# Four graph layers on one core: the last slot and the drain of layers 0 to 2 written as one list of steps, with the first two attention units of layer 3 inside it

## The chip, the core and the metric

The kernel runs on one core of a Trainium2 chip. The metric is the device time of one execution in microseconds; the median of three runs before the change is 2056.01 us (2053.41 to 2056.41). A compute core has five engines that run beside each other, each through its own list of instructions in order: TensorE (PE, matrix products into PSUM, with its weight loads shown as PEld), VectorE (DVE), ScalarE (ACT), GpSimd (POOL) and SyncE (SP), which here only starts transfers.

## The reference

Input x is 32 graphs of 512 nodes with 64 features, adj a sparse symmetric 512 x 512 matrix. Four layers follow each other, each of the form x = x + layer(relu(layernorm(x))):

```python
# layer 0: h = relu(layernorm(x))
out = h @ w_self + (adj @ h) @ w_neighbor + bias
# layer 1: z = h, then twice
z = relu((adj @ z) @ weights[i])
# layer 2: graph attention with e1_i + e2_j as its scores
Wh = h @ W.T;  e = leaky_relu(e1[:, None] + e2[None, :], 0.2)
out = elu(softmax(where(adj > 0, e, NEG)) @ Wh)
# layer 3: 8 attention heads, then one more attention over all heads
def gat_layer(x, graph, W, b):
    h = x @ W
    s = (h @ h.T) * graph
    s = where(s == 0, -1e16, s)
    return softmax(s) @ h + b
cat = leaky_relu(concat(heads), 0.01)
out = leaky_relu(gat_layer(cat, adj, W_out, b_out), 0.01)
```

Everything is float32.

## The kernel before, in words

All of x lies in SBUF. Work has two parts. **Layers 0 to 2** go by blocks: a block is two graphs, and there are 16 of them (M = 16). **Layer 3** goes by units of two attention matrices: 128 `Heads` units (one graph, two heads) and 16 `Out` units (two graphs), 144 in all.

*Layers 0 to 2.* `slot(k)` (L1134) holds one step of several blocks at once: layer 0 of block k, the first half of layer 1 of block k-2, its second half for block k-3 (`ends`), and of layer 2 the flip and preparation of block k-4 and the scores and products of block k-5. PE, DVE and ACT run in the order in which the code is written, by `manual_schedule`. The names that matter, with the lines where they are in the profile:

- nt (L930): the product with adj, four matmuls of 512 columns, copied out by ACT (L937). One is layer 0's (nt0), two are layer 1's (nt1, then nt1b with z).
- po (L950): products with the small weights (po0, po1a, po1b). z is relu of po1a.
- `centre` (L869, L871) takes off the mean; the square is taken on ACT (L890), its sum on DVE (var, L908), the root on ACT (L915), and `relu` (L894) applies it.
- `Gat` (L959): flip (L318, a transpose, copied to ht at L320), e_ps and wh_ps (L973, L982), their exponentials on ACT (v, q and c, L993 to L999), weigh (L1004), scores (s, L1014), acc and den (L1027, L1036), kept (two copies on ACT, L1046), back (two groups of transposes, den_ps and op_ps, L1058 and L1063), read (L1073 to L1076), exp (e, L1083), and rest (L1089 to L1092), which adds to x and takes the mean and square for layer 3.

In the first slots a set-up step of its own is run at a slot's end (`begun`, L1336): `gat_weights`, edges, masks, `flow_weights`, `scales`, and then checks of adj row by row (`judge_rows`, `count_rows`, `judge`), which lead to the flag that chooses the general form.

Slot 16 is the last. `drain` (L1224) then ends blocks 12 to 15, written by hand, with 36 recorded products of `fill` (L1222), whose result nobody reads, and with the first periods of layer 3's preparation (-10 to -2) between.

*Layer 3.* `period(t)` (L743 and on, made by `planned`) does for each unit a step that depends on its age: the scores s_ps (L391) of rows 2 and 3 of unit t and of rows 0 and 1 of unit t+1; the maxima (L403, which also copy to p_att); the row maximum sent to memory and back to all partitions (top_row, topb: L410, L418, on SP); the shift by it on POOL (L424, L428); the exponential (L437); the join of two rows (L440, DVE); the totals (tot_ps, L458); the products (av, L446); the reciprocals, sent round in the same way (recb); normalise (L495); and the output steps. p_att has a ring of 14 tiles. The ring, the row tiles and the PSUM pools are opened when the pools of layers 0 to 2 are closed. In period 1 the shift runs on DVE.

Of the kernel before, what the change touches and what calls it, by code (L numbers as in the profile page):

```python
# [10 lines left out]
OP = mybir.AluOpType  # L11
# [11 lines left out]
def fast_form(  # L23
# [48 lines left out]
    early = ctx.enter_context(tc.tile_pool(name="early", bufs=1))  # L72
    setup_ctx = ExitStack()
    setup = setup_ctx.enter_context(tc.tile_pool(name="setup", bufs=1))
    adj_p = setup.tile([P, C, C, P], F32, name="adj_p")
# [94 lines left out]
    def scales():  # L170
        own = tiny.tile([P, C], F32, name="own_edge")
        for c in range(C):
            d = row_pair("d")[:, 0, :P]
            nc.vector.scalar_tensor_tensor(
                d, adj_p[:, c, c], 1.0, ident, op0=OP.mult, op1=OP.mult,
                accum_out=own[:, c : c + 1],
            )
        nc.vector.tensor_scalar(sound[:, 2 : 2 + C], own, 1e-20, None, op0=OP.is_gt)
        nc.vector.tensor_scalar(own, own, 1e-20, None, op0=OP.max)

        root = tiny.tile([P, C], F32, name="root")
        nc.scalar.activation(root, own, AF.Sqrt)
        nc.vector.reciprocal(root_d, root)
        nc.vector.tensor_tensor(root_d, root_d, own, OP.mult)
        nc.vector.tensor_tensor(root_d, root_d, root, OP.add)
        nc.vector.tensor_scalar(root_d, root_d, 0.5, None, op0=OP.mult)
        ones = row_pair("ones")[:, 0, :P]
        nc.vector.memset(ones, 1.0)
        ps = acc("urow_ps", [P, N])
        for c in range(C):  # L190
            d = row_pair("d")[:, 0, :P]
            nc.vector.tensor_scalar(d, ident, root_d[:, c : c + 1], None, op0=OP.mult)
            nc.tensor.matmul(
                ps[:, c * P : (c + 1) * P], lhsT=ones, rhs=d, start=True, stop=True
            )
        nc.scalar.copy(urow, ps)
# [3 lines left out]
    def judge_rows(c):  # L200
        both = judged[c] = row_pair("edge")
# [32 lines left out]
    def row_pair(name):  # L234

        return pairs_of[0].tile([P, 2, N], F32, name=name, tag="row")


    acc_of, pairs_of = [], []
# [4 lines left out]
    def judge():  # L244
        counts = sound[:, 2 + C :]
        nc.vector.tensor_scalar(counts, counts, float(N), None, op0=OP.is_equal)
        own = tiny.tile([P, 1], F32, name="own")
        nc.vector.tensor_reduce(own, sound, AX.X, OP.min)
        ps = acc("own_ps", [1, P])
        nc.tensor.transpose(ps, own, ident)  # L250
        nc.vector.tensor_reduce(unsound, ps, AX.X, OP.min)
# [14 lines left out]

    def gat_weights():
# [6 lines left out]
        wa = setup.tile([P, 2], F32, name="wa")  # L274
# [3 lines left out]
        size = tiny.tile([P, 2], F32, name="size")  # L278
        nc.vector.scalar_tensor_tensor(size, wa, -1.0, wa, op0=OP.mult, op1=OP.max)

        pz = acc("size_ps", [P, 2])
# [5 lines left out]

    def flow_weights():
        whT = pairs_of[0].tile([P, H, 2, F], F32, name="whT", tag="row")
# [3 lines left out]
        for k in range(2):  # L293
            nc.scalar.copy(whT[:, :, k], pt)
        pm = acc("m2_ps", [P, H, F])
# [12 lines left out]
        nc.scalar.mul(bh01, pb, 0.01)  # L308
        nc.vector.tensor_reduce(
# [16 lines left out]

    LATE = 7
# [6 lines left out]
    class Pair:  # L334
# [4 lines left out]
        def begin(self):  # L339
            self.p = {}  # L340
# [45 lines left out]
        def scores(self, r):  # L386
            g, x = self.terms()
            ps = ps_s.tile([P, 2, N], F32, name="s_ps", tag="s")
            self.s_ps[r] = ps
            for k in range(2):  # L390
                nc.tensor.matmul(  # L391
                    ps[:, k], lhsT=x[halves(k), r * P : (r + 1) * P], rhs=g[halves(k), :],
# [3 lines left out]
        def maxima(self, r):  # L396
# [3 lines left out]
            self.p[r] = pbuf.tile([P, 2, N], F32, name="p_att")  # L400
            for k in range(2):
                at = k * C + r
                nc.vector.tensor_tensor_reduce(  # L403
                    out=self.p[r][:, k], in0=ps[:, k], in1=flow_neg[:, r], scale=-1.0,
# [10 lines left out]
        def spread_in(self):  # L415
            self.topb = wk.tile([P, 2, N], F32, name="topb")
# [16 lines left out]
        def exps(self, r):  # L433
            to = self.p[r]
            if r % 2:
                to = self.joined = ps_s.tile([P, 2, N], F32, name="e_ps", tag="s")
            nc.scalar.activation(to, self.p[r], AF.Exp, scale=-1.0)  # L437

        def join(self, r):
            nc.vector.tensor_tensor(self.p[r], self.joined, self.p[r - 1], OP.add)  # L440
# [296 lines left out]
    def planned(units, products):  # L737
# [7 lines left out]
        def period(t):  # L745
# [3 lines left out]
            now, ahead = unit(0), unit(-1)  # L749
# [5 lines left out]
            if t != 1:  # L755
                unit(1).shift(0, nc.gpsimd)
                unit(1).exps(0)
            unit(2).totals()
            unit(2).totals_out(1, nc.scalar)
# [3 lines left out]
            if t != 1:  # L763
                unit(1).shift(2, nc.gpsimd)
                unit(1).exps(2)
# [3 lines left out]
            unit(2).totals_out(0, nc.sync)  # L769
# [8 lines left out]
            if t == 1:  # L778
                for r in (0, 2, 1, 3):
                    unit(1).shift(r, nc.vector)  # L780
                    if r < 3:
                        unit(1).exps(r)
# [3 lines left out]
            if t != 1:  # L786
                unit(1).shift(1, nc.gpsimd)
                unit(1).exps(1)
            for j in range(C):
                unit(2).values(j)  # L790
# [5 lines left out]
            unit(1).join(1)  # L796
            if t != 1:
                unit(1).shift(3, nc.gpsimd)
            unit(1).exps(3)
            unit(5).back_pool()  # L800
            unit(-2).make_gs()
            unit(1).join(3)
# [35 lines left out]
    assert not due and len(late) == LATE  # L838
    flow_period = planned(flow, products)
# [10 lines left out]
    with (  # L850
        tc.tile_pool(name="pairs_a", bufs=H + 3) as pairs,
# [83 lines left out]
        def copied(p, tag):  # L935
            t = work.tile([P, N], F32, name=tag, bufs=1 + (tag == "nt1b"))
# [3 lines left out]
        def flipped(h, tag):  # L940
            return pair_transpose(
# [998 lines left out]
```

## Time and profile before

| | us |
|---|---|
| median of three runs | 2056.01 |
| the profiled execution, its time | 2056.54 |
| its span, first to last instruction | 2054.7 |
| PE, DVE busy in the span | 1966.7, 1736.7 |
| POOL, ACT busy in the span | 1446.0, 1321.5 |
| PE, DVE busy of the first 362.2 | 331.2, 277.0 |

The page of the profile gives each engine's busy time for the whole span, then the span in 40 slices of about 51 us, each digit the busy tenths of an engine. Slices 1 to 9 are layers 0 to 2, the rest is layer 3. A second kind of row gives the same for stretches of one's own choice. A third lists instructions of one engine in order of time, with idle time ahead of one in brackets and who ended it. The clock row (PEclk) is the share of TensorE's full clock that was granted.

### The profile page before, as it was taken

Reading aid. Unit: us, or ns where it says so; the run is one execution under the profiler, and the core shown is the slowest. Engines: PE = TensorE matmul, PEld = TensorE weight load, DVE = VectorE, ACT = ScalarE, POOL = GpSimd, SP = SyncE. Lnnn points to the kernel's source line nnn. Section 1 sums busy time; section 2 is a strip of 40 time slices with the busy share of each in tenths; the row PEclk is TensorE's granted clock in tenths of the full one; section 3 lists DMA queues with packets and bytes.
Section 4 is the critical chain, followed back from the end, with each engine's and each line's share of the span. In section 5 each row is a group of like instructions: output and inputs, shape, how many; then the busy total and the mean of one; then the engine's idle time right before and its main releaser. Section 6 shows DMA issues by size and latency. Waiting matters only on the chain.

```text
span 2054.7 us, 29214 instructions
## 1 busy us (share of the span) xinstructions
PE 1966.7 (96%) x9374; PEld 738.0 (36%) x9374; DVE 1736.7 (85%) x4107; ACT 1321.5 (64%) x2008; POOL 1446.0 (70%) x834
## 2 busy tenths in 40 slices
PE   7999999887999999999999999999999999999995
PEld 4555555432333333333333333333333333333332
DVE  5688887678889898888898888888888888888994
ACT  3444444445676777677676777777777776776674
POOL 2000000005898989898999999898898988889996
PEclk9999999999999999999999999999999999999998
DMA  4000000002222333223332323232322222222233
GB/s 122 1 1 1 1 1 1 1 0 53 79 74 71 82 79 80 79 74 79 79 79 75 84 79 79 69 84 74 76 72 78 74 71 77 79 74 76 72 83 80
DMA packets 185875, 128.05 MB, mean 62 GB/s; under 512 B 124984, under 2 KB 130272, under 8 KB 185584
## 3 DMA queue, kind: packets, MB, share of 16 engines
q1 hardware_dynamic: 166480, 125.30, 22.9%
q10 hardware_dynamic: 18720, 0.59, 0.5%
q8 instruction: 76, 1.25, 0.3%
q14 instruction: 87, 0.71, 0.1%
q0 software_dynamic: 512, 0.20, 0.1%
HBM read 119.48 MB, written 5.37 MB: 61 GB/s over the span
## 4 chain that ended last, share of the span: by engine, by line
PE 75%; DVE 8%; POOL 6%; ACT 5%; DMA 4%; issue 2%; SPq 0%; ACTq 0%; POOLq 0%; DVEq 0%
PE s_ps L391 22%; PE av L446 20%; PE tot_ps L458 6%; PE y_ps L576 5%; POOL p_att L424 5%; PE gT_ps L621 5%; PE nt_ps L930 4%; PE g_ps L558 3%; PE acc L1027 3%; DVE s L1014 2%; DMA topb<-top_row 2%; PE den L1036 1%; DVE p_att L403 1%; PE po L950 1%; DVE p_att L440 1%
## 5 line engine op out<-in xcount | busy, mean ns | idle before, releaser
L424 POOL TENSOR_TENSOR p_att<-p_att,topb 128x1024 f32<-128x1024 f32 x429 | 1008.0, 2381 | 0.0
L403 DVE CUSTOM_DVE_ANT_0 p_att<-s_ps,flow_neg 128x512 f32<-128x512 f32 x1152 | 726.1, 686 | 99.8 <-PE s_ps L391 98.2
L391 PE MATMUL s_ps<-g,hx 64*128 64x512 f32 x2048 | 516.3, 613 | 16.8 <-DVE p_att L440 14.8
L428 POOL TENSOR_TENSOR p_att<-p_att,topb 128x512 f32<-128x512 f32 x286 | 360.4, 1281 | 168.8 <-DMA topb<-top_row 112.5
L437 ACT ACTIVATE p_att<-p_att 128x1024 f32<-128x1024 f32 x288 | 304.8, 1059 | 164.4 <-POOL p_att L428 83.9
L440 DVE TENSOR_TENSOR p_att<-e_ps,p_att 128x1024 f32<-128x1024 f32 x288 | 338.7, 1198 | 31.1 <-ACT e_ps L437 30.5
L437 ACT ACTIVATE e_ps<-p_att 128x1024 f32<-128x1024 f32 x288 | 292.9, 1029 | 79.7 <-POOL p_att L424 74.2
L391 PEld LDWEIGHTS s_ps<-g,hx 64*128 64x128 f32 x2048 | 175.3, 186 | 329.8 <-DVE top L403 174.1
L446 PE MATMUL av<-p_att,hd 128*64 128x512 f32 x1024 | 269.7, 605 | 0.5 <-DVE o_att L495 0.3
L446 PE MATMUL av<-p_att,hn 128*64 128x512 f32 x1024 | 263.3, 592 | 0.0
L1138 POOL TENSOR_TENSOR x<-x,bias_b 128x512 f32<-128x512 f32 x16 | 20.4, 1277 | 292.3 <-DVE hn L871 292.3
L594 DVE SCALAR_TENSOR_TENSOR cat<-y_ps,bh,cat 128x512 f32<-128x512 f32 x256 | 180.1, 745 | 14.2 <-ACT cat L586 12.8
L570 ACT COPY g<-g_ps 128x512 f32<-128x512 f32 x128 | 131.7, 1137 | 85.8 <-PE g_ps L558 85.7
L586 ACT ACTIVATE cat<-y_ps,bh 128x512 f32<-128x512 f32 x256 | 161.4, 682 | 36.4 <-PE y_ps L576 35.7
L458 PE MATMUL tot_ps<-p_att,ones 128*32 128x512 f32 x1152 | 156.4, 608 | 4.0 <-DVE p_att L440 4.0
L576 PE MATMUL y_ps<-o_att,wh_sb 64*128 64x512 f32 x512 | 137.3, 594 | 0.0
L621 PE MATMUL gT_ps<-cat,wo_sb 128*64 128x512 f32 x512 | 131.6, 592 | 0.0
L446 PEld LDWEIGHTS av<-p_att,hn 128*64 128x64 f32 x1024 | 73.9, 137 | 145.9 <-issue 145.9
L446 PEld LDWEIGHTS av<-p_att,hd 128*64 128x64 f32 x1024 | 62.4, 136 | 165.8 <-issue 134.2
L495 DVE TENSOR_TENSOR o_att<-av,recb 128x512 f32<-128x512 f32 x144 | 99.1, 688 | 26.5 <-DMA recb<-rec_row 22.7
L930 PE MATMUL nt_ps<-adj_t,hn 128*128 128x512 f32 x256 | 118.8, 608 | 0.8 <-DVE hn L894 0.8
L464 ACT COPY tot<-tot_ps 128x512 f32<-128x512 f32 x144 | 83.2, 578 | 32.3 <-PE tot_ps L458 31.5
(193 smaller groups left out, 2088.0 us busy)
## 6 DMA issues: line engine op xcount, KB each, us to landing
topb<-top_row SPq DMA_DIRECT2D x288, 256.0 KB
recb<-rec_row SPq DMA_DIRECT2D x288, 128.0 KB
out_dram<-y SPq DMA_DIRECT2D x32, 128.0 KB
x<-in_x_dram SPq DMA_DIRECT2D x3, 1024.0 KB
top_row<-top SPq DMA_DIRECT2D x144, 4.0 KB
parts<-tot SPq DMA_DIRECT2D x144, 4.0 KB
parts<-tot ACTq DMA_DIRECT2D x144, 4.0 KB
rec_row<-rec_flow SPq DMA_DIRECT2D x144, 4.0 KB
```

The costliest lines, as they stand in the source:

```text
L391: nc.tensor.matmul(ps[:, k], lhsT=x[halves(k), r * P : (r + 1) * P], rhs=g[halves(k), :], start=True, stop=True,)
L403: nc.vector.tensor_tensor_reduce(out=self.p[r][:, k], in0=ps[:, k], in1=flow_neg[:, r], scale=-1.0, scalar=BIG, op0=OP.add, op1=OP.min, ac ...
L424: engine.tensor_tensor(self.p[r], self.p[r], self.topb, OP.subtract)
L428: engine.tensor_tensor(p, p, self.topb[:, k], OP.subtract)
L437: nc.scalar.activation(to, self.p[r], AF.Exp, scale=-1.0)
L440: nc.vector.tensor_tensor(self.p[r], self.joined, self.p[r - 1], OP.add)
L446: nc.tensor.matmul(self.av[halves(k), :], lhsT=self.v(k, j) if j % 2 else self.less_next(k, j), rhs=self.p[j][:, k], start=(j == 0), stop= ...
L458: nc.tensor.matmul(ps[q : q + 32, :], lhsT=ones, rhs=self.p[2 * e + 1][:, k], start=True, stop=True,)
L576: nc.tensor.matmul(ps, lhsT=wh_sb[halves(k), 2 * self.i + k, :], rhs=self.o[halves(k), :], start=True, stop=True,)
L594: nc.vector.scalar_tensor_tensor(self.cat[:, k], self.y[k], bh[:, h : h + 1], self.cat[:, k], op0=OP.add, op1=OP.max,)
L621: nc.tensor.matmul(self.gps[halves(k), :], lhsT=wo_sb[:, h, :], rhs=Heads.cat.pop((self.b + k, h)), start=(h == 0), stop=(h == H - 1),)
L930: nc.tensor.matmul(p, lhsT=lhs(k), rhs=adj_t[:, k, :], start=(k == 0), stop=(k == C - 1))
```

## The change

Four things change together.

1. *Set-up in steps.* `gat_weights`, `scales`, `flow_weights` and `judge` are cut where a product needs what DVE or ACT has just made, and the second piece runs a slot later: `gat_sizes` in slot 1, `own_edges` in 2, `roots` in 3, `roots_row` and `flow_squares` in 4, `flow_least` in 5; `judge_counts` in 13, `judge_across` in 14, and the end of `judge` within slot 15.
2. *Inside a slot* the product with z is issued ahead of `back`, and ACT copies nt0 ahead of the square of the second norm.
3. *The list.* Slots run from 0 to 15. What slot 16 and `drain` did is a string of step names, taken one after the other; `fill` is gone. In it stand, of units 0 and 1 of layer 3, the scores (s0 to s3), maxima (m), spread, shifts on POOL (sh), exponentials (ex) and joins (j). Periods -11 to -1 run at the ends of slots 10 to 14. After the list come the totals of unit 0, period 1, its products, period 2, the last root of layer 2, and periods from 3 on; periods leave out what the list did, and in period 3 the shift of rows 1 and 3 is on DVE.
4. *Lasting memory.* Eight of the 14 p_att tiles are held from the start: six tiles `row0` to `row5`, and adj_p as two. Set-up steps use them as scratch. The rows of layer 2 have pools of their own (s: four, c: two, e: one) instead of eleven shared; topb of units 0 and 1 is in adj_t, and their scores are in the PSUM pool of layers 0 to 2, in two banks each.

```diff
+    lasting = [keep.tile([P, 2, N], F32, name=f"row{i}") for i in range(6)]
+    adj_p = keep.tile([P, C, C, P], F32, name="adj_p")
+    lasting += [
+        adj_p.rearrange("p c k q -> p c (k q)")[:, c : c + 2] for c in range(0, C, 2)
+    ]
...
+    EARLY = 2
+    RING = 4 * C - 2
...
+            at = (C * self.at + r) % RING
+            self.p[r] = (
+                lasting[at] if at < len(lasting) else pbuf.tile([P, 2, N], F32, name="p_att")
+            )
...
+            if self.at < EARLY:
+                self.topb = adj_t[:, 2 * self.at : 2 * self.at + 2]
...
-            to = self.p[r]
-            if r % 2:
-                to = self.joined = ps_s.tile([P, 2, N], F32, name="e_ps", tag="s")
+            to = self.joined[r] = self.p[r]
+            if r % 2 and self.at >= EARLY:
+                to = self.joined[r] = ps_s.tile([P, 2, N], F32, name="e_ps", tag="s")
...
+            now, ahead, last = (unit(i) if t - i >= EARLY else nothing for i in (0, -1, 1))
+            summed = unit(2) if t > 2 else nothing
...
             n = make(n2, k - 3)
             if n:
                 n.a()
-                n.square()
                 some.append(n)
             if l0:
                 nt0 = copied(neighbours(lambda c: h0[:, c]), "nt0")
+            if n:
+                n.square()
...
+            if l1:
+                nt1b[k - 2] = neighbours(lambda c: z[:, c, :])
             if u:
                 u.back()
                 turned.append(u)
-            if l1:
-                nt1b[k - 2] = neighbours(lambda c: z[:, c, :])
-            if more:
-                more()
+            for step in more:
+                step()
...
+        LAST = """
+        grow_15 nt1bc_13 flip_12 nt1_14 ht_12 read_10 sc0_11 exp_10 po1b_13 nt1c_14 rest_10
+        e1_12 wh_12 c_12 po1a_14 vq_12 n1_15 s0_0 z_14 osq_10 sc1_11 sq1_15 x_13 acc_11
+        n2_13 var1_15 sq2_13 weigh_12 var2_13 den_11 kacc_11 ovar_10 m0_0 root_0 op_11
+        nt1b_14 sc0_12 kden_11 turn_0 dps_11 relu1_15 nt1bc_14 s1_0 relu2_13 nt1_15 m1_0
+        read_11 sc1_12 exp_11 flip_13 nt1c_15 po1b_14 ht_13 e1_13 rest_11 wh_13 c_13 acc_12
+        vq_13 x_14 osq_11 n2_14 den_12 ovar_11 sq2_14 weigh_13 kacc_12 var2_14 s2_0 kden_12
+        sc0_13 root_1 dps_12 s3_0 po1a_15 m2_0 op_12 z_15 m3_0 nt1b_15 turn_1 relu2_14
+        read_12 sc1_13 flip_14 nt1bc_15 spread_0 s0_1 ht_14 exp_12 po1b_15 e1_14 x_15 acc_13
+        rest_12 c_14 n2_15 osq_12 den_13 sh0_0 kacc_13 ovar_12 sq2_15 m0_1 op_13 kden_13
+        sh1_0 ex0_0 dps_13 var2_15 s1_1 read_13 root_2 s2_1 m1_1 sh2_0 m2_1 s3_1 period_0
+        exp_13 sh3_0 turn_2 ex2_0 wh_14 m3_1 vq_14 relu2_15 spread_1 ex1_0 sc0_14 flip_15
+        ht_15 ex3_0 weigh_14 sc1_14 e1_15 wh_15 c_15 vq_15 sh0_1 rest_13 acc_14 sh1_1 ex0_1
+        weigh_15 osq_13 j3_0 den_14 kacc_14 sh2_1 ovar_13 ex1_1 op_14 sc0_15 kden_14 dps_14
+        sh3_1 ex2_1 sc1_15 ex3_1 read_14 j3_1 exp_14 acc_15 rest_14 den_15 kacc_15 j1_0
+        osq_14 ovar_14 op_15 kden_15 j1_1 dps_15 read_15 exp_15 rest_15 osq_15
+        """
...
+            for step in LAST.split():
+                name, i = step.split("_")
+                do[name](int(i))
...
+            for k, step in (
+                (0, gat_weights), (1, gat_sizes), (1, edges), (2, masks), (2, own_edges),
+                (3, flow_weights), (3, roots), (4, roots_row), (4, flow_squares),
+                (5, flow_least),
+            ):
+                begun[k].append(step)
...
+            for k, some in (
+                (10, (-11, -10, -9)), (11, (-8, -7)), (12, (-6, -5)), (13, (-4, -3)),
+                (14, (-2, -1)),
+            ):
+                for t in some:
+                    begun[k].append(lambda t=t: flow_period(t))
+            for k in range(M):
+                slot(k, begun[k])
+            unfinished = drain()
...
-        for k in range(-1, len(flow) + ROOM):
+        flow[0].totals()
+        flow[0].totals_out(1, nc.scalar)
+        flow[0].totals_out(0, nc.sync)
+        flow_period(1)
+        for j in range(C):
+            flow[0].values(j)
+        flow_period(2)
+        end_of_gat(unfinished)
+        for k in range(3, len(flow) + ROOM):
             flow_period(k)
```

In a step name the number is that of the block, or of the unit for s, m, spread, sh, ex and j. acc and op are one half of values and back, den and dps the other; kacc and kden copy them; x is the end of layer 1; ovar is the sum of rest's square; ending c is the copy of a product (nt1c, nt1bc); osq is the square.

## The prediction

> **What bounds the kernel now.** I read the 40 slices first (how busy each engine is, stretch by stretch), then a table of four stretches, then the waits and the order of time inside the stretches that the change touches.
>
> ```profile
> PE   7999999887999999999999999999999999999995
> PEclk9999999999999999999999999999999999999998
> ...
> 362.23:485.62 123.39, 97.29 (x462) 43.92 (x461) 89.98 (x188) 58.90 (x125) 4.57 (x5) 0.93 0.03 9
> 506.10:2054.70 1548.60, 1517.76 (x7161) 501.23 (x7159) 1354.46 (x3284) 1091.44 (x1563) 1395.67 (x783) 1.00 0.30 77
> ```
>
> The last two rows are stretches, with the busy time of PE, PEld, DVE, ACT and POOL, then clock, DMA share and GB/s. Layer 3 from 506 us on is TensorE's: 1517.8 of 1548.6 us, at full clock. It stays as it is: by the instruction order of both kernels, compared engine by engine with the names of the probability tiles set aside, the periods after the fourth are the same on PE, ACT and SP, and on Pool but for some waits on PE. So the gain must come from the first 510 us. The worst stretch is 362 to 486 (slot 16, drain, first periods of layer 3): PE 79%, DVE 73%, nobody full.
>
> The waits of 100 to 362 us (who waited for whom; us, times, longest), then matmuls in order of time (start, length, operation, and in brackets the idle time before them):
>
> ```profile
> PE den_ps L1058 <- ACT kept L1046: 7.8, 11, 0.7
> PE wh_ps L982 <- ACT nt L937: 6.1, 10, 0.6
> ...
> 58.82 2.00 PE L297 MATMUL m_ps<-whT 128*128 128x64 f32 x16 [1.16 <-ACT whT L294]
> 60.90 5.40 PE L930 MATMUL nt_ps<-adj_t,hn 128*128 128x512 f32 x8
> 67.90 3.60 PE L930 MATMUL nt_ps<-adj_t,hn 128*128 128x512 f32 x8
> 83.34 2.04 PE L193 MATMUL urow_ps<-d,ones 128*128 128x128 f32 x8 [3.63 <-DVE d L192]
> ...
> 398.24 5.40 PE L930 MATMUL nt_ps<-adj_t,z 128*128 128x512 f32 x8 [2.68 <-ACT c L999]
> 485.62 3.79 PE L391 MATMUL s_ps<-g,hx 64*128 64x512 f32 x8 [8.23 <-DVE p_att L440]
> ```
>
> A full slot lasts 25.1 us and holds 23.8 us of PE; the 1.32 us missing are the first two waits. In set-up PE pays twice, once for the gap and once after it: the same nt_ps takes 5.40 instead of 3.60.
>
> **Set-up in steps.** Nothing is computed less; each product is put a slot behind its input. Slot 0's wait for size (1.03 idle, L282) goes. In slot 3, 1.16 idle goes, m_ps drops from 1.95 to about 0.95 (the 16 wh_ps products of 65 columns take 0.95 at full clock), nt_ps gives 1.8: 4.0. In slot 4, 3.63 idle goes, urow_ps falls from 1.84 to 0.9 (eight 128-column products of po1a take 0.9), nt_ps gives 1.7: 6.2. Sum 11.2 us. What took their place is ready: the next slot's DVE steps and copies lie a whole slot before the matmul that needs them. If one were late, its few-us gap returns.
>
> **Slots 5 to 15.** The product with z now stands ahead of back, so the copies of kept (0.59 each) lie under 3.44 us of matmul; the copy of nt0 stands ahead of the square, which waits for DVE. That frees 7.8 + 6.1 = 13.9. Is DVE the next bound? It has 21.9 busy in a judging slot. Its wait for e (2.7 of 25.1 us) shrinks, since nt1b, square, table load and exp start about 1.8 earlier; against it stands up to 0.8 at read, because op_ps comes later. I get 21.9 + 0.8 + 0.35 + 0.45 = 23.5 beside PE's 23.8: just hidden. If that cover fails by 0.3 it costs 8 x 0.3 = 2.4. Judge's 7.7 us wait on DVE goes too, off PE's path. Back on the bill: periods -11 to -1 move into slots 10 to 14. Their hx and g products are about 2 us of PE, and the last g copies (2 x 1.12 on ACT) stand ahead of slot 15's nt1b: about 1 us. The features (12 small ACT operations for each of graphs 0 and 1, 1.06 + 1.05 + 1.28 us, and hd on Pool) fit into ACT's half-empty slots. Net 13.9 - 3.0 = 10.9. So the point that lay at 362.2 comes at 340.1.
>
> **The planned list.** PE: four nt products 13.8, acc and den of five blocks 27.4, four of e and wh 7.7, back 4.7, po 4.5, flips 1.8, units 0 and 1's scores 7.5, g 1.0: 68.4 us. The 36 fill records (17.8 us) go. DVE has more: 89.98 of before, less the five DVE shifts (4.8), the four extra maxima (2.9), unsound, grow and least (1.5), plus two joins (2.4): 83.2 us. So DVE is the floor. I followed the list by hand, each step starting when its engine and inputs allow, lengths from the rows (s x4 2.65, rest 2.87, read 1.1, maxima 1.23, acc 3.6, table load 1.28, about 0.15 a hand-over). Two new orders bind it. The scores tiles s are now four of their own where eleven rows were shared, so the scores of one block wait for den of the block before: in a slot den ends at 281.7 and the scores begin at 292.2, 10 us of cover; in the list sc0_13 follows den_12 by a fraction of a us, and if PE is late there DVE waits with everything queued behind it (read, rest, maxima), us for us. And topb of units 0 and 1 goes into adj_t, which is free only after nt1b_15: spread_0 stands behind it, with 4 us between. DVE stands still at the start of block 14's weights (its q comes behind period 0's g copies, 2 to 3 us) and little elsewhere: 90 us to the last rest.
>
> A wait that before hardly shows: the eight shifts of units 0 and 1 go to Pool (2 x 1.28 + 3 x 2.38 = 9.7 us a unit), beside a dense DVE.
>
> ```profile
> 479.95 3.49 DVE L424 TENSOR_TENSOR p_att<-p_att,topb 128x1024 f32<-128x1024 f32 x3
> 482.42 3.37 POOL L428 TENSOR_TENSOR p_att<-p_att,topb 128x512 f32<-128x512 f32 x2 [28.48 <-DVE p_att L424]
> ```
>
> Pool's two operations take 3.37, not 2.52, exactly where DVE still runs one of the other row until 483.44: about 1 us of overlap cost Pool 0.86, DVE nothing (1.22 each throughout). The Trainium skill, GPSIMD Engine Reference, Specifications, says that Pool shares its SBUF interfaces with VectorE, in contention with DVE instructions that have two SBUF inputs; it names no price. By the profile's average row (2381 ns) the shifts would be free. With the rule, s, x, o, hn and the joins (about 51 of DVE's 83 us) lock Pool out, so 19.5 us of shifts need some 40 us, and unit 1's joins come late. When DVE waits for them Pool runs freely, so the loss limits itself. Ends 0 and 10; I take 5. List: 95 us.
>
> The fills speak of the clock. The Trainium skill, TensorE: Matmul & The Clock Gate, in its table for your kernels, wants no PE gap over about 3 us; the trace is stricter (1.16 idle behind small transposes gave the 5.40). By the rule nearly no gap in my walk counts; by the row perhaps four products are slowed by 1.9, 7.6 us of PE, of which 26 are spare beside DVE. I take 0, ends 0 and 5.
>
> **After the list.** Last rest to unit 2's totals: maxima of unit 2 (6), top_row and topb (2.8 + 3.3), Pool's and DVE's shifts, root, exponentials and joins of period 3: 25 us. SP has spreads 0 and 1 ahead of these in its queue and nothing else. Before, unit 2's totals stand at 510.4. Now: 340.1 + 95 + 25 = 460.1. Gain 50.3 (11.2 set-up, 10.9 slots, 28.2 drain and start). The profiled execution took 2056.54 (span 2054.7 plus 1.84 around it), the median of the runs is 2056.01: 2056.0 - 50.3 = 2005.7.
>
> **Rivals.**
> A. The likeliest, as above: 1994 to 2016. Chance 0.56.
> B. DVE stays the bound with its waits: slots keep most of their 25.1 and the list waits for chains as the old drain did (about 20 us more). For: DVE's 35 us idle in the old drain are waits on chains, and a list can only order them. Against: the longest chain, block 15's, is about 51 us, far below 95. Gain 20 to 35: 2021 to 2036. Chance 0.18.
> C. Pool isn't locked out and hand-overs are tighter: gain 58 to 66, 1990 to 1998. Chance 0.12.
> D. Slower: layer 3 falls into a worse phase. Periods start with other spacings, eight of 14 probability tiles lie in other memory, and the PSUM pools changed places; Pool is busy 90% there (1395.7 of 1548.6). The price repeats 141 times: from 50.3 / 141 = 0.36 us a period the gain is gone, at 0.45 the time is 2019. At 0.8: 2056 - 50 + 113 = 2119. Against: same order, same operands, PE full. Chance 0.09.
> E. It does little: the list's gain is eaten by Pool and clock, and the slots turn DVE-bound. 2040 to 2056. Chance 0.05, about half of it within 0.2% (4.1 us, about what a measurement of this kernel can tell from no change).
>
> **The numbers.** Likeliest 2005.7. From 1990 to 2033 lie A, C and most of B: about 0.83. Faster 0.89, same 0.03, slower 0.08 (D, less its mildest part).
>
> **What would show it.** Right: nt_ps of slots 4 and 5 at 3.6; slots of 23.8 with no PE wait for kept or nt; the list about 95 us, DVE nearly full; Pool's shifts in it well over 2381 ns; unit 2's totals near 460; layer 3 unchanged at some 1544 from there to the end. Wrong: slots above 24.5 with DVE full, DVE waits in the list above 15 us, or another period in layer 3.

## The result and the profile after

| | before | after |
|---|---|---|
| median, us | 2055.66 (4 runs, 2053.41 to 2056.41) | 2020.9 (4 runs, 2020.11 to 2021.3) |
| ratio of the times | 1 | 0.9832, 95% interval 0.9815 to 0.9849 |
| span of the profiled execution | 2054.7 | 2019.4 |
| first acc product (end of set-up) | 100.39 | 90.23 |
| first acc to the last in a slot (ten slots) | 251.15 | 240.16 |
| the point at 362.2, where the list starts | 362.23 | 340.24 |
| end of the list (last mean of rest) | | 446.5 |
| totals of unit 2 | 510.36 | 475.42 |
| from there to the end | 1544.34 | 1543.98 |

The kernel is 34.8 us faster where 50.3 were forecast. All that is missing lies between 340 and 475 us: the list is 11.3 longer than forecast and its way to unit 2's totals 3.9.

The 40 slices of the changed kernel, then its stretches (list, start, layer 3; columns as for before):

```profile
PE   7999999868999999999999999999999999999995
POOL 2000000226989999989898989898898888889996
PEclk9999999888999999999999999999999999999998
```

```profile
340.24:446.50 106.26, 85.30 (x430) 38.45 (x430) 97.20 (x172) 47.34 (x84) 22.11 (x10) 0.89 0.03 11
446.50:475.42 28.92, 20.38 (x81) 6.10 (x77) 20.29 (x54) 14.30 (x25) 13.17 (x8) 0.86 0.21 56
475.42:2019.40 1543.98, 1516.48 (x7153) 501.68 (x7151) 1350.95 (x3278) 1088.01 (x1557) 1386.21 (x778) 1.00 0.29 77
```

But for the list's first 13 us, list and start lie in the eighth to tenth slices (353 to 505 us): PE stands at 8, 6 and 8 there. Pool's 2 and 2 tenths in the eighth and ninth are new; the 6 of the tenth was a 5 before. Layer 3 keeps its length. In the list DVE is busy for 97.20 us where my sum had 83.2, with the same instructions. Only the time of each can have grown. DVE in order of time shows where (start, length, operation):

```profile
384.21 1.44 DVE L1157 SCALAR_TENSOR_TENSOR x<-o,x 128x512 f32<-128x512 f32 x1
385.76 1.58 DVE L1158 SCALAR_TENSOR_TENSOR x<-e,x 128x512 f32<-128x512 f32 x1
...
388.10 4.24 DVE L907 SCALAR_TENSOR_TENSOR o<-sum,x 128x256 f32<-128x256 f32 x2
392.25 0.67 DVE L905 TENSOR_REDUCE sum<-x 128x8 f32<-128x512 f32 x1
392.96 2.20 DVE L907 SCALAR_TENSOR_TENSOR hn<-sum,x 128x256 f32<-128x256 f32 x2
...
409.81 6.84 DVE L1069 SCALAR_TENSOR_TENSOR s<-c,q,mask 128x512 f32<-128x512 f32 x4 [5.07 <-ACT q L1041]
416.58 0.74 DVE L1057 TENSOR_TENSOR v<-wh_ps,v 128x256 f32<-128x256 f32 x2
417.25 6.26 DVE L1069 SCALAR_TENSOR_TENSOR s<-c,q,mask 128x512 f32<-128x512 f32 x4
...
425.59 0.76 DVE L907 SCALAR_TENSOR_TENSOR o<-sum,x 128x256 f32<-128x256 f32 x2
```

The same pair o<-sum,x takes 4.24 at 388 and 0.76 at 425; four scores take 6.84 and 6.26, elsewhere 2.73; x takes 1.44 and 1.58, elsewhere 0.69. The excess of the stretched rows is 14.2 us. Not stretched are a reduction with one input (0.67) and v, which has one input in PSUM (0.74). The stretched ones all read two tensors from SBUF, and they lie exactly beside Pool's shifts of units 0 and 1:

```profile
383.83 2.96 POOL L468 TENSOR_TENSOR row<-row,adj_t 128x512 f32<-128x512 f32 x2 [66.73 <-DMA adj_t<-top_row]
386.76 7.79 POOL L464 TENSOR_TENSOR row<-row,adj_t 128x1024 f32<-128x1024 f32 x3
410.23 3.13 POOL L468 TENSOR_TENSOR row<-row,adj_t 128x512 f32<-128x512 f32 x2 [15.69 <-DMA adj_t<-top_row]
413.32 2.79 POOL L464 TENSOR_TENSOR row<-row,adj_t 128x1024 f32<-128x1024 f32 x1
416.07 5.56 POOL L464 TENSOR_TENSOR adj_p<-adj_p,adj_t 128x1024 f32<-128x1024 f32 x2
```

Pool itself took 22.1 us for these shifts instead of 19.5. So the two engines do shut each other out, but the one that stands is DVE.

The slots and set-up did as forecast. In the waits of 100 to 350 us no row of PE for kept or nt is left, and what x waits for e shrank from 32.1 us to:

```profile
DVE x L1158 <- ACT e L1151: 15.5, 10, 6.7
...
PE nt_ps L966 <- DVE unsound L272: 2.9, 1, 2.9
PE nt_ps L966 <- ACT g L610: 1.1, 1, 1.1
```

The last two rows are new and lie in slot 15, which takes in judge's end and the g copies. Eight slots are 23.35 us long from acc to acc (acc at 113.58, 136.93, 160.28), the one after them is 24.22, slot 15 is 29.13.

### The profile page after: what moved, and what is told of

The parts are those of the page before. It is cut to its first block, busy times and chain, and to the rows that moved or that the text cites. A ratio compares the mean times of both kernels' runs of the same rounds, so it can differ in the third digit from the quotient of the medians.

```text
span 2019.4 us, 29031 instructions
## 1 busy us (share of the span) xinstructions
PE 1946.5 (96%) x9338; PEld 729.7 (36%) x9338; DVE 1747.8 (87%) x4104; ACT 1320.8 (65%) x2008; POOL 1452.9 (72%) x837
## 4 chain that ended last, share of the span: by engine, by line
PE 79%; POOL 7%; DVE 6%; DMA 4%; ACT 2%; issue 1%; SPq 0%; ACTq 0%; POOLq 0%; DVEq 0%
PE s_ps L425 22%; PE av L486 20%; PE nt_ps L966 8%; PE tot_ps L498 6%; PE y_ps L616 5%; PE gT_ps L661 5%; PE g_ps L598 3%; POOL p_att L464 3%; PE acc L1082 2%; DMA topb<-top_row 2%; POOL row L464 2%; PE po L988 1%; DVE s L1069 1%; PE den L1093 1%; DVE p_att L440 1%
## 5 line engine op out<-in xcount | busy, mean ns | idle before, releaser
L464 POOL TENSOR_TENSOR row<-row,topb 128x1024 f32<-128x1024 f32 x182 | 430.5, 2388 | 0.0
L464 POOL TENSOR_TENSOR p_att<-p_att,topb 128x1024 f32<-128x1024 f32 x182 | 429.6, 2383 | 0.0
L440 DVE CUSTOM_DVE_ANT_0 p_att<-s_ps,flow_neg 128x512 f32<-128x512 f32 x492 | 310.0, 686 | 43.7 <-PE s_ps L425 42.8
L440 DVE CUSTOM_DVE_ANT_0 row<-s_ps,flow_neg 128x512 f32<-128x512 f32 x496 | 312.5, 685 | 39.1 <-PE s_ps L425 38.9
L468 POOL TENSOR_TENSOR p_att<-p_att,topb 128x512 f32<-128x512 f32 x124 | 155.6, 1277 | 94.4 <-DMA topb<-top_row 80.5
L468 POOL TENSOR_TENSOR row<-row,topb 128x512 f32<-128x512 f32 x120 | 150.9, 1279 | 63.8 <-DMA topb<-top_row 49.3
L477 ACT ACTIVATE p_att<-p_att 128x1024 f32<-128x1024 f32 x123 | 130.2, 1058 | 69.8 <-POOL p_att L468 35.6
L480 DVE TENSOR_TENSOR p_att<-e_ps,p_att 128x1024 f32<-128x1024 f32 x123 | 145.5, 1198 | 15.8 <-ACT e_ps L477 15.3
L480 DVE TENSOR_TENSOR row<-e_ps,row 128x1024 f32<-128x1024 f32 x121 | 143.2, 1197 | 13.9 <-ACT e_ps L477 13.4
L477 ACT ACTIVATE e_ps<-p_att 128x1024 f32<-128x1024 f32 x123 | 125.7, 1029 | 39.1 <-POOL p_att L464 33.0
```

Source lines behind the costliest of these rows:

```text
L440: nc.vector.tensor_tensor_reduce(out=self.p[r][:, k], in0=ps[k], in1=flow_neg[:, r], scale=-1.0, scalar=BIG, op0=OP.add, op1=OP.min, accum ...
L464: engine.tensor_tensor(self.p[r], self.p[r], self.topb, OP.subtract)
L468: engine.tensor_tensor(p, p, self.topb[:, k], OP.subtract)
L480: nc.vector.tensor_tensor(self.p[r], self.joined.pop(r), self.p[r - 1], OP.add)
```

## The experiments

Two kinds of number are compared: the ratio to before on the same chip, and points inside the profiled executions (list start, list length, start, unit 2's totals). From one chip to another the medians of before differ by 4 us, so small differences are read from the points. What follows unit 2's totals is the same work in every run and took 1542.5 to 1550.6 us in these executions, so that a time can move by some us without its points.

| run | list start | list | start | unit 2's totals | median | ratio, 95% interval |
|---|---|---|---|---|---|---|
| after | 340.2 | 106.3 | 28.9 | 475.4 | 2020.9 | 0.9832 [0.9815, 0.9849] |
| after_again | 340.1 | 106.1 | 28.9 | 475.1 | 2021.69 | 0.9834 [0.9812, 0.9855] |
| after_third | 343.7 | 105.7 | 31.3 | 480.7 | 2028.1 | 0.9842 [0.9829, 0.9856] |
| shift_left_out | 340.9 | 90.7 | 29.2 | 460.8 | 2012.24 | 0.9774 [0.9757, 0.9792] |
| shift_on_dve | 343.1 | 98.2 | 29.1 | 470.4 | 2020.29 | 0.9805 [0.9785, 0.9825] |
| root_late | 340.4 | 99.2 | 28.4 | 468.0 | 2018.89 | 0.9827 [0.9805, 0.9848] |
| unit1_late | 340.2 | 98.0 | 33.2 | 471.3 | 2016.5 | 0.9809 [0.9787, 0.983] |
| g_late | 340.5 | 94.6 | 31.6 | 466.7 | 2016.08 | 0.9789 [0.9776, 0.9803] |
| fills_back | 340.8 | 106.5 | 29.4 | 476.8 | 2024.58 | 0.9831 [0.9816, 0.9846] |
| setup_merged | 348.4 | 106.3 | 29.1 | 483.9 | 2036.57 | 0.9895 [0.9878, 0.9911] |
| slot_order_back | 361.9 | 104.7 | 29.1 | 495.6 | 2044.89 | 0.9927 [0.9911, 0.9944] |
| pool_two_inputs | 376.2 | 105.4 | 31.3 | 512.8 | 2058.86 | 1.0016 [1.0006, 1.0025] |
| pool_one_input | 349.1 | 105.6 | 31.5 | 486.2 | 2036.9 | 0.9889 [0.9871, 0.9907] |

The first theory was that the 11 us missing in the list are Pool's shifts, which hold up DVE's operations with two SBUF inputs. Its rivals were the clock (the fills are gone), and chains that DVE waits for whatever Pool does.

### The shifts left out

```diff
-                do[f"sh{r}"] = lambda i, r=r: flow[i].shift(r, nc.gpsimd)
+                do[f"sh{r}"] = lambda i, r=r: None
...
-            nc.scalar.activation(to, self.p[r], AF.Exp, scale=-1.0)
+            nc.scalar.activation(
+                to, self.p[r], AF.Exp, scale=-1e-3 if self.at < EARLY else -1.0
+            )
```

> The eight shifts of units 0 and 1 are left out altogether, and the exponential of these two units takes a small factor so that it stays finite; all else stays, so the time is that of the list without Pool's work (the result of the softmax of these two units is not that of the reference). Theory 1: the list falls by the excess of 14.2 us and by the waits that follow from it, to 86-92 us; time 2001-2007. Theory 2: the list stays at 103-106 us, time 2018-2021, since Pool's work is beside the others'.

The list, from its start to the last mean of rest:

```profile
340.87:431.60 90.73, 80.82 (x430) 36.16 (x430) 82.86 (x172) 47.60 (x84) 0.00 (x0) 0.94 0.05 13
```

DVE has the same 172 instructions as in the changed kernel and is busy for 82.86 us instead of 97.20. My sum had 83.2 of DVE and a walk of 90: both stand, to 0.7 us, once Pool is silent. Pool's 22 us of shifts cost the list 15.5 us. Two things changed besides: the granted clock is 0.94 instead of 0.89, and the chain through the shifts (row maximum sent round, shift, exponential, join) is cut. The next run keeps that chain, and the fills put back, below, test the clock.

### The shifts on DVE

```diff
-                do[f"sh{r}"] = lambda i, r=r: flow[i].shift(r, nc.gpsimd)
+                do[f"sh{r}"] = lambda i, r=r: flow[i].shift(r, nc.vector)
```

> The eight shifts of units 0 and 1 in the list run on DVE instead of Pool; nothing else changes. Theory 1 (Pool and DVE exclude each other: in the list of after, DVE operations with two inputs in SBUF took 14 us too long while Pool shifted): the excess of 14.2 us and most of DVE's 5.1 us wait for q go, 9.9 us of shifts come to DVE (2 x 0.69 + 3 x 1.22 a unit, twice), so the list falls from 106 to 95-100 us and the time to 2011-2017. s x4 takes 2.7 again, not 6.8. Rival theory 2 (the list is long because of its chain of hand-overs and the half clock of TensorE): DVE only gets 10 us more to do, time 2025-2031.

```profile
343.07:441.30 98.23, 84.43 (x430) 36.80 (x430) 91.91 (x182) 47.88 (x84) 0.00 (x0) 0.91 0.05 12
```

DVE does 9.05 us more work than without the shifts (91.91 less 82.86) and the list is still 8 us shorter than with them on Pool. The chain through the shifts is whole here, so it was not what made the list long. The busiest engine gains by taking work over from one that was idle.

### Two inputs against one, beside a DVE that has work

To measure the disputed cost by itself, twenty needless Pool operations of 128 x 1024 were put into the queue of the slots: in one kernel with two tensors from SBUF, in the other with one.

```diff
+                if 5 <= k < 15:
+                    for _ in range(2):
+                        nc.gpsimd.tensor_tensor(
+                            lasting[0], lasting[0], flow_neg[:, 0:2], OP.mult
+                        )
```

```diff
+                if 5 <= k < 15:
+                    for _ in range(2):
+                        nc.gpsimd.tensor_scalar(
+                            lasting[0], lasting[0], 1.0, None, op0=OP.mult
+                        )
```

> After, plus twenty operations on Pool that nobody needs (row0 = row0 x flow_neg, 128x1024, two inputs in SBUF, 2.38 us each) in the stretch of slots 4 to 7, where the changed kernel has no Pool work but one short addition a slot. Theory 1 (exclusion): DVE's operations with two inputs in SBUF stretch there as in the list (s x4 from 2.7 to 5-7 us), DVE becomes the bound, and 48 us of Pool cost 10-30 us. Theory 2 (Pool beside DVE costs nothing; the list was long for other reasons): time as after within 2 us.

> The control for the twenty needless two-input Pool operations: the same twenty places in the slots, the same 128 x 1024 output, but a multiplication by a constant, so that Pool reads one SBUF input. If it is Pool's second SBUF input that shuts VectorE's two-input operations out, nothing is stretched: hn by rstd of slot 4 near 2.1 instead of 13.84, slots at 24.0, time that of the changed kernel, 2019 to 2024. If it is Pool's mere presence in SBUF, the stretch is about the same as with two inputs: 2050 to 2060.

With two inputs the time is 2058.86 us (ratio to before 1.0016, 95% interval 1.0006 to 1.0025), about 37 more than the changed kernel has, where I had expected 10 to 30, and the list starts 36 us later. They ran earlier than planned, since nothing held Pool back. Pool first, then DVE:

```profile
67.15 24.56 POOL L1214 TENSOR_TENSOR row<-row,flow_neg 128x1024 f32<-128x1024 f32 x10
```

```profile
68.34 13.84 DVE L931 SCALAR_TENSOR_TENSOR hn<-hn,rstd 128x256 f32<-128x256 f32 x6
...
84.64 2.20 DVE L199 TENSOR_SCALAR root_d<-root_d 128x4 f32<-128x4 f32 x1
...
86.90 5.09 DVE L202 TENSOR_SCALAR row<-ident,root_d 128x128 f32<-128x128 f32 x4
...
105.13 2.10 DVE L931 SCALAR_TENSOR_TENSOR hn<-hn,rstd 128x256 f32<-128x256 f32 x6
```

Ten Pool operations take 2.46 each. The six DVE operations beside them take 2.31 each (13.84 by six), 0.35 when Pool is silent: one DVE operation for each of Pool's. Also stretched were operations that read a single tensor: a multiplication by a constant of only 128 x 4 elements (2.20; 0.17 in the changed kernel) and four of 128 x 128 by a column of factors (5.09; 0.86). So two SBUF inputs of DVE are not the only case; in the list no such operation met Pool.

With one input, Pool and then DVE:

```profile
65.83 14.22 POOL L1214 TENSOR_SCALAR row<-row 128x1024 f32<-128x1024 f32 x5
```

```profile
54.87 2.94 DVE L931 SCALAR_TENSOR_TENSOR hn<-hn,rstd 128x256 f32<-128x256 f32 x6
...
65.89 0.69 DVE L1224 TENSOR_TENSOR x<-x,po 128x512 f32<-128x512 f32 x1 [5.18 <-POOL x L1217]
...
78.20 2.10 DVE L931 SCALAR_TENSOR_TENSOR hn<-hn,rstd 128x256 f32<-128x256 f32 x6
```

The six by rstd take 2.94 and 2.10, both beside Pool's one-input operations (the 0.84 is one operation that took 1.26 instead of 0.42), and the four multiplications of 128 x 128 take 1.73: little beside 13.84 and 5.09. The time did not come back to that of the changed kernel, as I had expected: 2036.9 us (ratio 0.9889, 0.9871 to 0.9907), 8.8 more than after_third on the same chip. That is another cost, in the second line: layer 0's bias waits in Pool's queue behind the needless operations, and DVE waits 5.18 for it. So of the 37 us some 9 are probably the queue, and the rest, some 28, the contention with the two-input operations; this split is worked out, not measured by itself. The two kernels differ in the kind of Pool's operation (tensor_tensor, tensor_scalar) as well as in its inputs, and which of the two decides was not separated.

### Unit 1 held back

Unit 0's shifts on DVE, unit 1's on Pool, but behind a one-column copy of a result of block 14, and with their exponentials and joins after the list.

```diff
+        nc.gpsimd.tensor_copy(held_one, unfinished.var[:, 1, 0, :1])
+        for r in (0, 2, 1, 3):
+            flow[1].shift(r, nc.gpsimd)
```

> Unit 0's shifts on DVE; unit 1's shifts stay on Pool but are held back (by a one-column copy that reads the sum of block 14) until DVE is nearly through the list, and its exponentials and joins follow behind unit 0's totals. Theory 1 (exclusion of Pool and DVE): the list falls from 106 to 92-95 us, since DVE gets 5 us of shifts, loses 2.4 us of joins and meets no Pool; the start grows by 0-4 us. Ratio to before 0.977-0.980. Rival: what the list gains the start loses, because unit 1's totals and products then wait for Pool: 0.983.

The list's last means on DVE:

```profile
426.91 0.76 DVE L908 SCALAR_TENSOR_TENSOR o<-sum,x 128x256 f32<-128x256 f32 x2
...
433.91 4.24 DVE L908 SCALAR_TENSOR_TENSOR o_end<-sum,x 128x256 f32<-128x256 f32 x2
```

The list is as long as with all shifts on DVE (98.0, where I had expected 92 to 95), in part because the tail of block 15 still meets Pool: 4.24 again. And the start is 4 us longer, as unit 1's totals now wait. Moving the clash moves a part of the cost: of 8.3 us that the list gains over the changed kernel the start gives 4.3 back. The ratio, 0.9809, lies between my theory's (to 0.980) and the rival's (0.983).

### Root after period 3

For the 3.9 us of the start my theory was the last root of layer 2: DVE waits 3.16 for it, and period 3 is behind. All shifts on DVE and the root behind period 3:

```diff
+        flow_period(3)
         end_of_gat(unfinished)
-        for k in range(3, len(flow) + ROOM):
+        for k in range(4, len(flow) + ROOM):
```

> As shift_on_dve (the eight early shifts on DVE), and the last root of layer 2 (the sum over o_end, ACT's table load and root, DVE's reciprocal) after period 3 instead of ahead of it. In after DVE stood 3.2 us for that root with the maxima of unit 3 and 4 and the DVE shifts of unit 2 queued behind it. Theory: the start from the last rest to unit 2's totals falls from 29 to 25-26 us, so 3-4 us below shift_on_dve (ratio to before about 0.979). Rival: the shifts of unit 2 wait for topb and Pool anyway, and nothing changes (0.9805).

The start is 28.4, not 25 to 26. The wait for the root is gone, and this stands in its place:

```profile
456.32 0.69 DVE L535 TENSOR_TENSOR o_att<-av,recb 128x512 f32<-128x512 f32 x1 [5.03 <-DMA recb<-rec_row]
```

That theory fell: the start is 0.7 us shorter, not 3 to 4. DVE now waits for the reciprocals of unit 0, sent round through memory, behind which the root had stood. The ratio, 0.9827, is no better than with the shifts on DVE alone.

### Fills put back

```diff
-        ht_15 ex3_0 weigh_14 sc1_14 e1_15 wh_15 c_15 vq_15 sh0_1 rest_13 acc_14 sh1_1 ex0_1
+        fill_6 ht_15 ex3_0 weigh_14 sc1_14 e1_15 fill_4 wh_15 c_15 vq_15 sh0_1 rest_13 acc_14 sh1_1 ex0_1
```

> The changed kernel with ten recorded-and-unread products of 512 columns put into TensorE's two longest gaps of the list: six ahead of the e product of block 15 (gap 5.66), four ahead of its wh products (gap 3.49). Left out or changed in the result: nothing. The clock rival says: e, wh and the first acc after these gaps ran at half clock (2.08, 2.30 and 6.07 where 1.13, 1.10 and 3.65 are their lengths at full clock), 4.6 us in all, so the list ends 3 to 5 us earlier, near 442.5, and the time falls to about 2016.5. My theory says: VectorE never waits in brackets behind these products between 417 and 446, so these three fall to their full-clock lengths and the list's end stays at 446.5 within 0.5, time 2020 to 2022.

```profile
413.36 3.70 PE L1415 MATMUL fill_ps<-mask,ident 128*128 128x512 f32 x8
416.99 1.11 PE L1025 MATMUL wh_ps<-wgv,ht 64*128 64x65 f32 x16
418.03 1.93 PE L1082 MATMUL acc<-s,v 128*64 128x512 f32 x6
420.99 1.08 PE L1082 MATMUL acc<-s,v 128*64 128x512 f32 x4 [1.03 <-DVE s L1069]
423.75 3.62 PE L1082 MATMUL acc<-s,v 128*64 128x512 f32 x6 [1.68 <-DVE s L1069]
```

The e product ahead of these falls from 2.08 to 1.13, wh from 2.30 to 1.11, and acc, instead of running 6.07 without a break, stops twice for the scores, which DVE delivers no sooner. The list is 106.5 long: nothing gained. The medians on this chip (2024.58 here, 2028.1 for after_third) differ by 3.5 us with ranges that overlap, and the points place that difference outside the list: 2.8 of it at its start already. So leaving out the fills cost nothing in the list, and the clock is not what made it long.

### Set-up merged

```diff
-                (0, gat_weights), (1, gat_sizes), (1, edges), (2, masks), (2, own_edges),
-                (3, flow_weights), (3, roots), (4, roots_row), (4, flow_squares),
-                (5, flow_least),
+                (0, gat_weights), (0, gat_sizes), (1, edges), (2, masks),
+                (3, flow_weights), (3, flow_squares), (3, flow_least),
+                (4, own_edges), (4, roots), (4, roots_row),
```

> The set-up steps are put back as in the kernel before: gat_sizes in slot 0 behind gat_weights, squares and least in slot 3, own edges, roots and their row all in slot 4. The rest is as after. My prediction's sum for this part: 11.2 us; the first acc came 10.2 us earlier in after than in before. Expected: 2030-2032. If the slots that follow hide part of it, 2021-2026. m_ps at 2.0 us, urow_ps at 2.0 and the nt_ps behind each at 5.4 again, instead of 3.6-3.7.

```profile
59.34 2.00 PE L323 MATMUL m_ps<-row 128*128 128x64 f32 x16 [1.16 <-ACT row L318]
...
82.27 1.49 PE L208 MATMUL urow_ps<-row,row 128*128 128x128 f32 x8 [3.74 <-DVE row L201]
```

The two gaps of before return, 1.16 and 3.74, and the first acc comes 8.2 us later (98.4), as does the list. Forecast for the steps were 11.2; before and after differ by 10.2 there. The half clock did not return in full: behind the gap of 1.16 nt_ps takes 3.70 here and 5.40 in before, behind the longer one 4.97. So what a gap costs after it is not fixed by its length. The ratio is 0.0063 above the changed kernel's, some 13 us of time where the points show 8; the intervals leave about 5 us either way.

### Order inside the slot undone

```diff
+                n.square()
                 some.append(n)
             if l0:
                 nt0 = copied(neighbours(lambda c: h0[:, c]), "nt0")
-            if n:
-                n.square()
...
-            if l1:
-                nt1b[k - 2] = neighbours(lambda c: z[:, c, :])
             if u:
                 u.back()
                 turned.append(u)
+            if l1:
+                nt1b[k - 2] = neighbours(lambda c: z[:, c, :])
```

> Within the slots the two orders of before are put back: back ahead of the product with z, the square ahead of the copy of nt0. The rest is as after. The prediction's sum: 13.9 us of waits return over slots 5 to 15, so 2032-2035, with slots of 25.1 us instead of 24.0. If DVE and not PE set the length of the slots in after, less comes back: 2023-2029.

The waits of 90 to 362 us:

```profile
PE den_ps L1118 <- ACT kept L973: 7.8, 11, 0.7
...
PE wh_ps L1025 <- ACT nt L973: 6.0, 9, 1.1
```

The 13.8 us are the 7.8 and 6.1 of before. The list starts 21.6 us later, more than these waits. From acc to acc the first eight slots are 25.11 us again instead of 23.35 (14.1 in all), the next is 2.3 longer and slot 15 is 3.8 longer; 3.1 of that is one nt product that ran at half clock behind the wait for judge (6.76 instead of 3.70), as it did by chance in an execution of the changed kernel too. The time, 2044.89, is above the 2032 to 2035 that I expected, and the ratio is 0.0095 higher, some 19 us. So the order is worth its 13.8 us of waits and more; the rest was not taken apart.

### The changed kernel again, and the late g copies

With the shifts on DVE a single wait of DVE above 1 us was left in the list: 3.67 for q, behind unit 2's g copies on ACT. I moved period 0, which makes them, from ahead of block 14's exponentials to behind block 15's.

```diff
-        ... m2_1 s3_1 period_0
+        ... m2_1 s3_1
...
-        ht_15 ex3_0 weigh_14 sc1_14 e1_15 wh_15 c_15 vq_15 sh0_1 rest_13
+        ht_15 ex3_0 weigh_14 sc1_14 e1_15 wh_15 c_15 vq_15 period_0 sh0_1 rest_13
```

> The changed kernel once more, unchanged, beside the others of this call on one chip. Both theories: its ratio to before again 0.983, list 106 us, unit 2's totals at 475.

> The changed kernel once more, on the chip of the three others, so that the gain of the late g copies and the price of the clock are differences on one chip: list 106.2, unit 2's totals at 475.4, ratio to before 0.983.

> All eight shifts of units 0 and 1 on VectorE, and period 0 (unit 2's g product and its two copies, four small feature operations on ScalarE) moved from ahead of block 14's exponentials to behind block 15's. In the kernel with the shifts on VectorE that is all that VectorE still waits for in the list: 3.67 for q at 407.6, with the two g copies (2.01) and the hs row (1.27) queued ahead on ScalarE. My theory: the wait falls to 0.5 or less, the list from 98.2 to about 95, unit 2's totals from 470.4 to about 467; time about 2013 to 2017, ratio to before 0.979 to 0.981. Rival: the wait only changes its releaser (the table load and e of block 12, 1.9 us, stand in the same queue): it stays above 2.5, totals at 469 to 470, ratio as with the shifts on VectorE alone.

```profile
340.62:435.16 94.54, 85.10 (x420) 37.08 (x418) 91.87 (x182) 48.06 (x84) 0.00 (x0) 0.88 0.05 12
435.16:466.71 31.55, 23.89 (x86) 7.05 (x84) 20.16 (x53) 14.30 (x25) 13.17 (x8) 0.82 0.20 51
```

The list falls to 94.6 as expected, DVE busy for 91.87 of it. The start is 31.6 here instead of 29.1, but that cannot be put down to the move. TensorE ran at half clock at its beginning, the scores ahead of it took 3.78 us instead of 1.99, and DVE waits 3.88 for the next. The unchanged kernel in after_third has the same there, a wait of 3.90 and a start of 31.3. First this run, then after_third:

```profile
431.67 3.78 PE L425 MATMUL s_ps<-g,hx 64*128 64x512 f32 x8 [0.82 <-DVE o_end L1144]
```

```profile
445.85 3.78 PE L425 MATMUL s_ps<-g,hx 64*128 64x512 f32 x8 [1.06 <-DVE o_end L1144]
```

So the 3.6 us by which the list is shorter than with the shifts on DVE are probably the gain, and the 3.7 by which unit 2's totals are earlier agree with it only by chance: 2.6 of them were there at the list's start. Against the changed kernel on the same chip this version takes 2016.08 us (2013.58 to 2019.95, five runs) where that takes 2028.1 (2025.18 to 2032.13, five runs): 12.0 us less, where unit 2's totals show 14.0 (3.2 of it at the list's start, ahead of the edits). It is faster than both kernels.

## Why the prediction held, and where it fell short

The sign and the place held, and of the terms set-up, slots, the walk, the clock and layer 3, some of them by errors that cancel. Pool's term was mis-sized, and the start left something out. The gain is 34.8 us, not 50.3, and the time lies in the gap between A (to 2016) and B (from 2021): inside the stated range because that was wide, not because the likeliest case came.

**Set-up:** 11.2 forecast, 10.2 by the point, 8.2 when that alone is undone. nt_ps of slots 4 and 5 take 3.70; no gap is left. One part of the sum was misread: m_ps was to drop from 1.95 to 0.95, as if it had run at half clock. With no gap ahead of it and at a granted clock of 1.00 it takes as long as before, and that is the size of the missing 1.0:

```profile
74.64 1.90 PE L323 MATMUL m_ps<-row 128*128 128x64 f32 x16
```


**Slots:** net 10.9 forecast; from the first acc to the last it is 11.0. That agreement is luck. The waits, 13.9, came back as 13.8, but a slot is 23.35, under the 23.8 that I took for PE's floor: 1.76 a slot instead of 1.32, 17.7 for ten. The bill was larger by as much: 6.7 instead of 3.0, of which 0.9 is in the slot before the last and 5.8 in slot 15 (29.13). I had judge's wait down as leaving PE's path; 2.9 us of it arrived on PE in slot 15, beside the 1.1 for the g copies that I had at about 1. The clock adds to it, differently from execution to execution. The product behind that wait, in the changed kernel, in after_third, and with the shifts on DVE:

```profile
321.99 3.70 PE L966 MATMUL nt_ps<-adj_t,hn 128*128 128x512 f32 x8 [2.94 <-DVE unsound L272]
```

```profile
322.48 6.63 PE L966 MATMUL nt_ps<-adj_t,hn 128*128 128x512 f32 x8 [2.95 <-DVE unsound L272]
```

```profile
323.23 5.29 PE L966 MATMUL nt_ps<-adj_t,hn 128*128 128x512 f32 x8 [2.95 <-DVE unsound L272]
```

The same gap gave full, half and mixed clock (granted 1.00, 0.54 and 0.69 over these products). That is 2.9 of the 3.4 us by which the list starts later in after_third, and 1.6 of 2.9 with the shifts on DVE.

**The list: this step failed, in its term for Pool beside DVE.** The prediction put it so: "DVE nothing", "lock Pool out, so 19.5 us of shifts need some 40 us", "Ends 0 and 10; I take 5". Measured are 15.5 us, outside my ends, and on the other engine: Pool needs 22.1 us and DVE stands for 14.2. The error is in how I read the row of before. There DVE's operation had been running when Pool's came, so Pool had to wait, and I took who waited in that one case for a rule. In the list Pool's operations follow each other almost without a gap, so each DVE operation comes while one of Pool's is running. The rows of before that I read had no such case, but the Trainium skill does: SBUF — State Buffer, Who interferes with whom, says that whichever of the two starts first keeps the shared pair for its whole instruction while the other blocks: "Issue order, not op shape, decides who blocks." With that rule, ten Pool operations would each hold up one DVE operation by up to Pool's length, an estimate of 0 to 19.5 us from the lengths of before, on the bound engine. This case's runs agree: one for one, 2.31 for a DVE operation beside Pool's 2.46.

The walk itself, 90, measures 90.7 without the shifts, although its one wait (q, forecast 2 to 3) was 4.8 and the others smaller; so that agreement is partly luck. Pool's cost gave the PE gaps, too: kept is late (3.58), ht (5.66), acc at half clock (6.07). These are followers; filling the two longest gained nothing. PE was busy for 85.3 us where my sum had 68.4, in part by the granted clock of 0.89; DVE, at 97.2, stayed the fuller engine. The clock's term, 0, held within the list; at slot 15 and at the start half clock took 2 to 3 us in single executions.

**After the list:** 25 forecast, 28.9 measured, and 28.4 to 29.4 in the other runs where the clock did not fall at its beginning (31.3 to 31.6 where it did; 33.2 with unit 1 held back). My sum left out unit 4's scores of row 3, which PE issues ahead of unit 2's totals and which wait for a join on DVE:

```profile
473.41 2.08 PE L425 MATMUL s_ps<-g,hx 64*128 64x512 f32 x4 [2.76 <-DVE p_att L480]
475.42 1.08 PE L498 MATMUL tot_ps<-p_att,ones 128*32 128x512 f32 x4
```

That the root makes it longer was not borne out (root_late). What binds it as a whole, joins, recb or both, stays open: it was not taken apart further.

**Layer 3:** 1543.98 after unit 2's totals against 1544.34, within the spread of the other runs (1542.5 to 1550.6, which was not explained). D, the slower rival, did not happen. B's number (2021 to 2036) is just missed by the median, but its reason is wrong: slots are at 23.35, and DVE stands idle for 9 us of the list, not 20. C fell with the 15.5.

## What to carry to other kernels

Work that is moved to an idle Pool is not free for VectorE if both read two tensors from SBUF (here some of VectorE's multiplications with one tensor were held up as well): charge VectorE with one Pool operation for each that it meets, or keep the work on VectorE when it is the bound, or give one of VectorE's two operands to PSUM. In costing a contention, ask who starts first in the new order, not who waited in the old trace. And a wait that is taken off the bound engine has to be followed to the next stage: here the late unit 1 gave half of its gain back within 30 us, and the late root put another wait in the place of the first. A stretch that looks longer after an edit has to be held against a second execution of the unedited kernel: the late g copies seemed to cost 2.5 us at the start, and the unedited kernel showed the same.

## What the runs showed of the hardware that I had not expected

- VectorE and Pool take turns by whole instructions: six VectorE operations of 0.35 us took 2.31 each beside Pool's 2.46, while Pool lost about 0.26 an operation in the list (22.1 instead of 19.5 for ten). A multiplication of 128 x 4 elements by a constant was held up as long as a large operation: 2.20 us instead of 0.17.
- It took a two-input operation on Pool: beside its multiplications by a constant, of 2.8 to 3.0 us each, the same six took 2.10 and 2.94 in all, instead of 13.84. The page named above speaks of any Pool operation that reads SBUF; here the measurement decides, for this kind of Pool operation.
- An operation with one input in PSUM was not held up, and layer 3 lives by it: its joins read e_ps from PSUM and take 1.2 us each while Pool is busy 90% of the time (1.22 in the list with both inputs in SBUF and Pool silent):

```profile
L480 DVE TENSOR_TENSOR p_att<-e_ps,p_att 128x1024 f32<-128x1024 f32 x123 | 145.5, 1198 | 15.8 <-ACT e_ps L477 15.3
```

- An idle TensorE of 2.94 us was followed by full clock in one execution (granted 1.00) and by half clock in another (0.54), and one of 1.16 us by half clock in before (5.40 for nt_ps) and by full clock with the set-up merged (3.70).
